# Weight taps and spectra on ScalarE's queue, x alone on SyncE's, and the gates' weight sums moved into the middle of the frequency phase

## The chip, the core and the metric

The kernel runs on one core of one Trainium2 chip. A core has five engines that run their own instruction streams in order and wait for one another through semaphores: TensorE (matrix products, PE in the profile), VectorE (DVE), ScalarE (ACT), GpSimd (POOL) and SyncE (SP), which only starts transfers. VectorE, ScalarE and GpSimd do elementwise work; SyncE and ScalarE can each start DMA transfers, and each has a DMA queue of its own. TensorE's results land in eight banks of PSUM, from which VectorE or ScalarE must copy them before a bank can be used again. The metric is the device time of one execution in microseconds (us); lower is better.

## What is computed

The input x is 128 graphs of 128 nodes with 256 channels. Only the first steps of the first layer touch the change:

```python
h = maximum(layernorm(x), 0)                    # per node
# inside the first layer, on h:
xc = transpose(h)                               # channels x nodes
c  = relu(bn1(conv1d(xc, conv1_w, pad=0)))      # 1-wide: a 256x256 product
c  = bn2(conv1d(c, conv2_w, pad=8))             # 17 taps over the nodes, 256 -> 256 channels
x_conv = transpose(relu(c + xc))
A = exp(-dist(h)) ; x_nmp = A @ relu(h @ w_msg + b_msg)
gi = concat(x_conv, x_nmp) @ w_ih.T ; gh = h @ w_hh.T
# a GRU cell on gi, gh; then x = x + result, and a second layer of five small graph convolutions
```

## The kernel before

**Blocks and halves.** The 128 graphs are worked on in 32 blocks of four (BB = 4), 16 blocks to a half. One block of x is 0.5 MB.

**The convolution by spectra.** The 17-tap convolution is done as a product in the frequency domain. A stretch of nodes is turned into 40 frequency pairs (LW = 80 values), and the 17 taps of each pair of channels too. For each pair p there is then one complex 256x256 product over all graphs of a half, written with three real products.

**The phases.** In order of time:

1. *Heads of half 0, interleaved with the weight spectra* (0 to 196 us). Eight weight spectra (2 parts of the input channels, 4 groups of 64 output channels) are made by `weight_spectra` in four steps each. In a step TensorE fills four PSUM banks (L160), of which ScalarE copies three (L168) and VectorE the fourth (L166) into the tile `sp`; after the fourth step `sp` (2.5 MB) is stored to `vd` in DRAM (L170). The taps of a spectrum are loaded by `taps_load` (L150) into the tile `w2`, 1 MB, of which there are two: those of spectrum k+2 can only be loaded when spectrum k has been through TensorE. Between the steps run the heads. For block i: its x load (L177, tile `ln`, five of them in half 0 and three in half 1), moments on VectorE (`head_stats`, L184, with a power on GpSimd at L189), normalisation on VectorE (`head_norm`, L195), transposes on TensorE (`head_turn`, L205, with relu to `ht` on ScalarE at L206, and a store `htd`, 0.5 MB, on ScalarE's queue at L207), the 1-wide convolution (`head_conv1`, L219; VectorE adds at L222, ScalarE does the relu at L223), and the transform to frequencies (`head_spectra`, L234; copies to X by VectorE at L240 and by ScalarE at L242).
2. *Frequency phase of half 0* (196 to 311 us), `spectral`: for each p, the spectra v are loaded from `vd` (L284, two loads of 0.5 MB for two frequencies, three such tiles), VectorE makes s (L297), GpSimd the sum vs of the real and imaginary parts (L299), TensorE does 12 matmuls (L302 and L307), ScalarE copies k1 (L304), VectorE adds (L308), and every four frequencies are stored to `yd` on ScalarE's queue.
3. *Heads of half 1* (311 to 426 us) and *frequency phase of half 1* (to about 540 us).
4. *The gates and the rest*, 540 us to the end.

**The gates' weight sums.** The gates use a product scheme with seven products in place of eight, for which sums of the blocks of the weights wih and whh are needed once, in `sw` and in place. `gate_weights` (L321 to L329) makes them as 12 additions on GpSimd; nothing needs them before the gates phase.

**What sets the order.** The program is written in one stream, and a scheduler with priorities gives each engine its own order when the kernel is built, and places the semaphores. An engine carries out its list in order, and a wait in it holds up what stands behind. Before the change, SyncE's order in the first phase is, for each spectrum k: the taps of k+2, the store of k, the x of block k+5. The 12 sums stand in GpSimd's order between vs of p = 3 and vs of p = 4.

Of the kernel before, what the change touches and what calls it, by code (L numbers as in the profile page):

```python
# [21 lines left out]
NP_ = LW // 2  # L22
WCH = 64
# [51 lines left out]
def gnn_kernel(ctx: ExitStack, tc: tile.TileContext, io, out0: bass.AP, out1: bass.AP):  # L75
    nc = tc.nc
# [15 lines left out]
    def bank():  # L92
        return psum.tile([P, 512], F32, tag="bank", name="bank")

    def row(name, n):

        return bass.AP(tensor=io[name].tensor, offset=io[name].offset, ap=[[0, P], [1, n]])
# [46 lines left out]
    vd = dram.tile([C, D // WCH, P, LW, WCH], F32, tag="vd", name="vd")  # L144
    yd = [dram.tile([HG, 2, LW, D], F32, tag=f"yd{h}", name=f"yd{h}") for h in range(NH)]

    def taps_load(pool, c, q, split=1):
        w2 = pool.tile([P, WCH // 4, P], F32, tag="w2", name="w2", bufs=2)
        for t in range(0, WCH // 4, WCH // 4 // split):
            nc.sync.dma_start(w2[:, t:t + WCH // 4 // split], io["w2t"][:, c, q, t:t + WCH // 4 // split])  # L150
        return w2

    def weight_spectra(pool, c, q, w2):

        sp = pool.tile([P, LW, WCH], F32, tag="sp", name="sp", bufs=2)
        for t in range(WCH // 16):
            ps = [bank() for _ in range(4)]
            for j in range(4):
                for r in range(4):
                    nc.tensor.matmul(ps[r][:, j * LW:(j + 1) * LW], w2[32 * r:32 * r + KW, 4 * t + j, :],  # L160
                                     gt[32 * r:32 * r + KW, :], start=True, stop=True)
            for r in range(4):
                o0 = t * 16 + 4 * r
                dst, s = sp[:, :, o0:o0 + 4], ps[r][:, :4 * LW].rearrange("p (j d) -> p d j", j=4)
                if r == 3:
                    nc.vector.tensor_copy(dst, s)  # L166
                else:
                    nc.scalar.copy(dst, s)  # L168
            yield
        nc.sync.dma_start(vd[c, q], sp)  # L170


    xs, stats, hcs, h1s = {}, {}, {}, {}
# [1 line left out]
    def head_load(pool, ahead, i, queue):  # L175
        xs[i] = pool.tile([P, BB, D], F32, tag="ln", name="ln", bufs=ahead)
        queue.dma_start(xs[i], x[i * BB:(i + 1) * BB].rearrange("b n d -> n b d"))  # L177
# [66 lines left out]
    def heads_begin(wk, xk, ahead, h):  # L244

        i = h * NBH
        for k in range(1 if h == 0 else 0, ahead):
            head_load(xk, ahead, i + k, nc.sync)
        for k in range(1 if h == 0 else 0, 3):
            head_stats(wk, i + k)  # L250
            if k < 2:
                head_norm(i + k)
        head_turn(wk, i)
# [20 lines left out]
    def spectral(bp, X, h, near_end):  # L274

        for p0 in range(0, NP_, 4):
            if p0 == NP_ - 8:
                near_end()
            ys = bp.tile([P, 4, 2, D], F32, tag="ys", name="ys", bufs=2)
            for p in range(p0, p0 + 4):  # L280
                if p % 2 == 0:
                    v = bp.tile([P, C, D // WCH, 4, WCH], F32, tag="v", name="v", bufs=3)
                    for c in range(C):
                        nc.sync.dma_start(v[:, c], vd[c, :, :, 2 * p:2 * p + 4, :].rearrange("q i d o -> i q d o"))  # L284
                vr, vi = v[:, :, :, 2 * (p % 2), :], v[:, :, :, 2 * (p % 2) + 1, :]
                a, d = X[:, :, p, 0, :], X[:, :, p, 1, :]
                y = ys[:, p - p0]
                ps = bank()
                if p == 0:
                    for k, (u, w) in enumerate(((a, vr), (d, vi))):  # L290
                        for c in range(C):
                            nc.tensor.matmul(ps[:, k * D:(k + 1) * D], u[:, c], w[:, c], start=c == 0, stop=c == C - 1)
                    nc.scalar.copy(y.rearrange("p k o -> p (k o)"), ps)
                    continue

                s = bp.tile([P, C, P], F32, tag="s", name="s", bufs=2)
                nc.vector.scalar_tensor_tensor(s, a, -2.0, d, op0=ALU.mult, op1=ALU.subtract)  # L297
                vs = bp.tile([P, C, D // WCH, WCH], F32, tag="vs", name="vs", bufs=3)
                nc.gpsimd.tensor_tensor(vs, vr, vi, op=ALU.add)  # L299
                p1 = bank()  # L300
                for c in range(C):
                    nc.tensor.matmul(p1[:, :D], a[:, c], vs[:, c], start=c == 0, stop=c == C - 1)  # L302
                k1 = bp.tile([P, D], F32, tag="k1", name="k1", bufs=2)
                nc.scalar.copy(k1, p1[:, :D])  # L304
                for k, (u, w) in enumerate(((s, vi), (d, vr))):
                    for c in range(C):
                        nc.tensor.matmul(ps[:, k * D:(k + 1) * D], u[:, c], w[:, c], start=c == 0, stop=c == C - 1)  # L307
                nc.vector.tensor_tensor(y, ps.rearrange("p (k o) -> p k o", k=2),  # L308
                                        k1[:, None, :].to_broadcast([P, 2, D]), op=ALU.add)
            for w in range(2):  # L310
                nc.scalar.dma_start(yd[h][:, w, 2 * p0:2 * p0 + 8, :].rearrange("g d o -> g (d o)"),
                                    ys[w * HG:(w + 1) * HG].rearrange("p a k o -> p (a k o)"))
# [18 lines left out]
    with front as es:  # L331
        hk = es.enter_context(tc.tile_pool(name="hk", bufs=1))
        xp = es.enter_context(tc.tile_pool(name="xp", bufs=1))
        X = xp.tile([P, C, NP_, 2, P], F32)
        with ExitStack() as ws:

            xk = ws.enter_context(tc.tile_pool(name="xk", bufs=1, side="right"))
            wp = ws.enter_context(tc.tile_pool(name="wp", bufs=1))
            ahead = 5
            todo = [(c, q) for c in range(C) for q in range(D // WCH)]  # L340
            head_load(xk, ahead, 0, nc.scalar)
            nc.sync.dma_start(gt, io["gt"])
            taps = [taps_load(wp, *todo[k], split=1 if k else 4) for k in range(2)]
            head_stats(hk, 0)
            head_norm(0)
            spectra = []

            def some_spectra(k=1):
                for _ in range(k):
                    if not spectra and todo:  # L350
                        spectra.append(weight_spectra(wp, *todo.pop(0), taps.pop(0)))
                    if spectra and next(spectra[0], STOP) is STOP:
                        spectra.pop(0)
                        if len(todo) > 1:
                            taps.append(taps_load(wp, *todo[1]))
                        some_spectra()

            some_spectra(3)
            constants()
            heads_begin(hk, xk, ahead, 0)  # L360
            some_spectra(3)
            heads(hk, xk, ahead, X, 0, lambda: some_spectra(2))
            while spectra or todo:
                some_spectra()
        gw = ctx.enter_context(tc.tile_pool(name="gw", bufs=1, side="right", reuse_waits="tile"))
        xk = es.enter_context(tc.tile_pool(name="xk1", bufs=1, reuse_waits="tile"))
        bp = es.enter_context(tc.tile_pool(name="bp", bufs=1, reuse_waits="tile"))
        idm = gw.tile([P, N], F32)
        wms = gw.tile([P, C, D + 3], F32)
        bms = gw.tile([P, D + 3], F32)  # L370
        wih = gw.tile([P, 2 * C, 3 * D], F32)
        whh = gw.tile([P, C, 3 * D], F32)
        sw = [gw.tile([P, 3, 3, P], F32, name=f"sw{k}") for k in range(3)]
        for h in range(NH):
            if h:
                heads(hk, xk, 3, X, h, lambda: None)
            spectral(bp, X, h, lambda: heads_begin(hk, xk, 3, h + 1) if h + 1 < NH else None)
            if h == 0:
                nc.sync.dma_start(idm, io["idm"])
                nc.sync.dma_start(wms, io["wms"].rearrange("(c p) o -> p c o", p=P))  # L380
                nc.sync.dma_start(bms, row("bms", D + 3))
                nc.sync.dma_start(fw, row("fw", 5))
                nc.sync.dma_start(wih, io["wih"].rearrange("(c p) o -> p c o", p=P))
                nc.sync.dma_start(whh, io["whh"].rearrange("(c p) o -> p c o", p=P))
                gate_weights()
# [718 lines left out]
```

## Time and profile before

Three runs took 1967.03, 1967.13 and 1971.97 us; the median is 1967.13 us. The profiled execution spans 1967.8 us.

| engine | busy us | share of the span |
|---|---|---|
| TensorE | 1911.4 | 97% |
| TensorE, weight loads | 1664.8 | 85% |
| VectorE | 1288.8 | 65% |
| ScalarE | 711.4 | 36% |
| GpSimd | 610.3 | 31% |

The share is an average over phases. TensorE is busy almost without a break from 540 us on; the page's second part, which cuts the span into 40 slices of 49.2 us, gives it 8, 8, 8 and 9 tenths in the first four slices and 7 in the seventh. In the same four slices the DMA engines are 8, 8, 8 and 5 tenths busy. In profile lines, a time in square brackets is how long the engine stood idle before the instruction, and the arrow names the instruction or the load that ended the wait. A row with "x4" joins four instructions of one kind. A row of SyncE's DMA queue (SPq) says when a transfer was started, not when it landed. TensorE's clock can be granted in full or in part; the same matmul then has a longer duration.

### The profile page before, as it was taken

Reading aid. Unit: us, or ns where it says so; the run is one execution under the profiler, and the core shown is the slowest. Engines: PE = TensorE matmul, PEld = TensorE weight load, DVE = VectorE, ACT = ScalarE, POOL = GpSimd, SP = SyncE. Lnnn points to the kernel's source line nnn. Section 1 sums busy time; section 2 is a strip of 40 time slices with the busy share of each in tenths; the row PEclk is TensorE's granted clock in tenths of the full one; section 3 lists DMA queues with packets and bytes.
Section 4 is the critical chain, followed back from the end, with each engine's and each line's share of the span. In section 5 each row is a group of like instructions: output and inputs, shape, how many; then the busy total and the mean of one; then the engine's idle time right before and its main releaser. Section 6 shows DMA issues by size and latency. Waiting matters only on the chain.

```text
span 1967.8 us, 29919 instructions
## 1 busy us (share of the span) xinstructions
PE 1911.4 (97%) x10418; PEld 1664.8 (85%) x10418; DVE 1288.8 (65%) x3255; ACT 711.4 (36%) x1438; POOL 610.3 (31%) x681
## 2 busy tenths in 40 slices
PE   8889997999999999999999999999999999999998
PEld 7778886998878888888878888888878888888887
DVE  6556445855468777777756677777756677777643
ACT  4444112531133433433434433333434433333334
POOL 1011641115423344344322143343322143343300
PEclk9899998999999999999999999999999999999999
DMA  8885795439863323323423533322423533322135
GB/s 312 324 290 179 229 314 183 164 123 293 282 197 84 90 67 92 89 69 79 121 59 98 129 107 83 95 71 70 123 71 94 130 94 94 84 71 56 51 90 148
DMA packets 248853, 265.76 MB, mean 135 GB/s; under 512 B 106850, under 2 KB 223927, under 8 KB 244223
## 3 DMA queue, kind: packets, MB, share of 16 engines
q1 hardware_dynamic: 240367, 225.58, 39.6%
q10 hardware_dynamic: 8336, 38.28, 5.1%
q8 instruction: 83, 1.36, 0.3%
q14 instruction: 67, 0.55, 0.1%
HBM read 178.66 MB, written 85.14 MB: 134 GB/s over the span
## 4 chain that ended last, share of the span: by engine, by line
PE 89%; DMA 5%; DVE 3%; POOL 1%; issue 1%; ACT 1%; SPq 0%; POOLq 0%; DVEq 0%; ACTq 0%
PE bank L565 44%; PE bank L307 6%; PE bank L471 6%; PE bank L884 5%; PE bank L824 5%; PE bank L219 5%; PE bank L302 3%; PE bank L517 3%; PE bank L453 3%; DMA ln<-in_x_dram 3%; PE bank L234 2%; PE bank L456 1%; PE bank L504 1%; PE bank L803 1%; PE bank L735 1%; PE bank L205 1%
## 5 line engine op out<-in xcount | busy, mean ns | idle before, releaser
L565 PE MATMUL bank<-t,sw 128*128 128x256 f32 x1152 | 290.7, 379 | 0.0
L578 POOL TENSOR_TENSOR u<-u,m 128x256 f32<-128x256 f32 x128 | 93.0, 726 | 595.2 <-ACT m L576 546.3
L565 PEld LDWEIGHTS bank<-t,sw 128*128 128x128 f32 x1152 | 215.6, 190 | 29.7 <-issue 2.3
L565 PE MATMUL bank<-t,wih 128*128 128x256 f32 x768 | 197.2, 379 | 0.0
L565 PEld LDWEIGHTS bank<-t,wih 128*128 128x128 f32 x768 | 143.4, 190 | 19.3 <-DVE u L583 0.5
L219 PE MATMUL bank<-wc,ht 128*128 128x256 f32 x512 | 130.0, 411 | 13.9 <-ACT ht L206 13.2
L299 POOL TENSOR_TENSOR vs<-v 128x512 f32<-128x512 f32 x78 | 101.1, 1315 | 130.1 <-DMA v<-vd 73.7
L219 PEld LDWEIGHTS bank<-wc,ht 128*128 128x128 f32 x512 | 103.7, 207 | 32.1 <-ACT ht L206 16.3
L471 PE MATMUL bank<-wms,ht 128*128 128x259 f32 x512 | 122.3, 381 | 0.0
L884 PE MATMUL bank<-w,hh 128*125 128x256 f32 (+9 forms) x480 | 113.6, 380 | 1.0 <-DVE hh L829 1.0
L565 PE MATMUL bank<-t,whh 128*128 128x256 f32 x384 | 114.4, 379 | 0.0
L565 PE MATMUL bank<-xn,wih 128*128 128x256 f32 x384 | 114.2, 379 | 0.0
L565 PE MATMUL bank<-xc,wih 128*128 128x256 f32 x384 | 114.2, 379 | 0.0
L297 DVE SCALAR_TENSOR_TENSOR s<-X 128x256 f32<-128x256 f32 x78 | 52.5, 675 | 91.9 <-PE bank L307 91.7
L565 PE MATMUL bank<-ht,whh 128*128 128x256 f32 x384 | 110.2, 381 | 0.0
L471 PEld LDWEIGHTS bank<-wms,ht 128*128 128x128 f32 x512 | 97.2, 190 | 14.6
L824 PE MATMUL bank<-ax,w 128*128 128x500 f32 (+8 forms) x416 | 107.0, 396 | 0.2 <-DMA w<-in_w_dram 0.2
L583 DVE TENSOR_TENSOR u<-bank,u 128x256 f32<-128x256 f32 x128 | 53.7, 419 | 74.0 <-PE bank L565 74.0
L189 POOL TENSOR_TENSOR rs<-ve,mhalf 128x4 f32<-128x4 f32 x32 | 32.3, 1009 | 225.2 <-DVE ve L187 225.2
L884 PEld LDWEIGHTS bank<-w,hh 128*125 128x125 f32 (+9 forms) x480 | 84.3, 178 | 19.3 <-DVE hh L829 1.6
L475 ACT ACTIVATE msg<-msg 128x512 f32<-128x512 f32 x64 | 40.3, 630 | 162.6 <-DVE msg L472 160.2
L304 ACT COPY k<-bank 128x256 f32<-128x256 f32 x78 | 28.9, 372 | 178.6 <-DVE ys L308 69.8
(190 smaller groups left out, 4307.1 us busy)
## 6 DMA issues: line engine op xcount, KB each, us to landing
v<-vd SPq DMA_DIRECT2D x80, 512.0 KB
vd<-sp SPq DMA_DIRECT2D x8, 2560.0 KB
yd<-ys ACTq DMA_DIRECT2D x40, 512.0 KB
w<-in_w_dram SPq DMA_DIRECT2D x40, 512.0 KB
htd<-ht ACTq DMA_DIRECT2D x32, 512.0 KB
ht<-htd SPq DMA_DIRECT2D x32, 512.0 KB
ym<-yd SPq DMA_DIRECT2D x32, 512.0 KB
xt<-in_xT_dram SPq DMA_DIRECT2D x32, 512.0 KB
```

Of the source, the lines that this page charges most:

```text
L219: nc.tensor.matmul(pv[:, bb, :], ht[:, c, b * N:(b + 1) * N], wc1[:, c, :], start=c == 0, stop=c == C - 1)
L299: nc.gpsimd.tensor_tensor(vs, vr, vi, op=ALU.add)
L302: nc.tensor.matmul(p1[:, :D], a[:, c], vs[:, c], start=c == 0, stop=c == C - 1)
L307: nc.tensor.matmul(ps[:, k * D:(k + 1) * D], u[:, c], w[:, c], start=c == 0, stop=c == C - 1)
L453: nc.tensor.matmul(ps[:, b * N:(b + 1) * N], ym[:, b, o * P:(o + 1) * P], idm, start=b == 0, stop=False)
L471: nc.tensor.matmul(ps[:, :D + 3], ht[:, c, b * N:(b + 1) * N], wms[:, c, :], start=c == 0, stop=c == C - 1)
L517: nc.tensor.matmul(ps[:, b * N:(b + 1) * N], msg[:, b, c * P:(c + 1) * P], e[:, b, :], start=True, stop=True)
L565: nc.tensor.matmul(ps, w, d, start=n == 0, stop=n == len(pairs) - 1)
L578: nc.gpsimd.tensor_tensor(got["u4"], got["u2"], got["m5"], op=ALU.add)
L583: nc.vector.tensor_tensor(got["u3"], ps, got["u2"], op=ALU.add)
L824: nc.tensor.matmul(pv[:, q - q0, :], w1s[k5 + g][:, c, q * P:(q + 1) * P], xv[:, c], start=c == 0, stop=c == C - 1)
L884: nc.tensor.matmul(ps[:n1, :D], hh[:, q, at:at + n1], w2s[k5 + g][:, q, :], start=q == 0, stop=q == HID // P - 1)
```

## The change

Four edits belong together.

1. `taps_load` is given a queue. The first two taps stay on SyncE, the other six go on ScalarE's queue.
2. The store of a spectrum goes on ScalarE's queue too. In the last step of each spectrum (t = 3) ScalarE now makes all four copies, so that the store on its queue waits for no copy by VectorE.
3. The first three x loads of half 1 go on ScalarE's queue. SyncE thus has x alone in the heads of half 0, and the loads of v behind it.
4. In half 0, at p = 20, three copies of one column of k1 into the tiles `sw` are put on GpSimd. The sums write the same elements, so they can only follow; this is a way to tell the scheduler that the sums come after p = 20. The columns are written over by the sums.

The aim of 1 to 3 is that an x block does not queue behind taps and stores; the aim of 4 is that the sums do not stand at the head of the frequency phase.

As built, SyncE's order has the x of blocks 1 to 13, the six loads of v for p = 0 to 5, and then the x of block 14. ScalarE's order has, per spectrum, the seven remaining copies, the two relu of `ht`, the store of the spectrum, the store `htd`, and the taps of the spectrum after next. GpSimd's order has vs of p = 25, the three copies, nine sums, vs of p = 26, two sums, vs of p = 27, and the last sum.

```diff
-    def taps_load(pool, c, q, split=1):
+    def taps_load(pool, c, q, queue, split=1):
         w2 = pool.tile([P, WCH // 4, P], F32, tag="w2", name="w2", bufs=2)
         for t in range(0, WCH // 4, WCH // 4 // split):
-            nc.sync.dma_start(w2[:, t:t + WCH // 4 // split], io["w2t"][:, c, q, t:t + WCH // 4 // split])
+            queue.dma_start(w2[:, t:t + WCH // 4 // split], io["w2t"][:, c, q, t:t + WCH // 4 // split])
...
-                if r == 3:
+                if r == 3 and t < WCH // 16 - 1:
                     nc.vector.tensor_copy(dst, s)
                 else:
                     nc.scalar.copy(dst, s)
             yield
-        nc.sync.dma_start(vd[c, q], sp)
+        nc.scalar.dma_start(vd[c, q], sp)
...
         for k in range(1 if h == 0 else 0, ahead):
-            head_load(xk, ahead, i + k, nc.sync)
+            head_load(xk, ahead, i + k, nc.scalar if h else nc.sync)
...
                 nc.scalar.copy(k1, p1[:, :D])
+                if h == 0 and p == NP_ // 2:
+
+                    for t in sw:
+                        nc.gpsimd.tensor_copy(t[:, 0, 1, 0:1], k1[:, 0:1])
...
-            taps = [taps_load(wp, *todo[k], split=1 if k else 4) for k in range(2)]
+            taps = [taps_load(wp, *todo[k], nc.sync, split=1 if k else 4) for k in range(2)]
...
-                            taps.append(taps_load(wp, *todo[1]))
+                            taps.append(taps_load(wp, *todo[1], nc.scalar))
```

## The prediction

> **What bounds the kernel now.** The page's first part has TensorE busy 97% of 1967.8 us. From about 540 us on, none of the changed lines runs, and TensorE has no gaps worth the name. So I read the first 310 us: first the table of 50 us stretches, whose columns are busy time and instruction count of each engine, granted clock, DMA share and GB/s.
>
> ```profile
> 0.00:50.00 50.00, 40.19 (x517) 35.44 (x518) 30.48 (x116) 21.55 (x54) 9.51 (x19) 0.93 0.90 311
> 50.00:100.00 50.00, 44.05 (x528) 39.04 (x527) 26.05 (x84) 23.37 (x67) 3.06 (x4) 0.86 0.86 328
> 100.00:150.00 50.00, 42.99 (x396) 38.30 (x395) 27.49 (x85) 21.88 (x58) 6.51 (x6) 0.93 0.81 288
> 150.00:200.00 50.00, 45.60 (x254) 40.31 (x253) 33.84 (x111) 19.40 (x53) 11.69 (x13) 0.93 0.45 160
> ```
>
> TensorE is idle 23 us of the first 150 while the transfers run at 0.8 to 0.9. To name the wait I took the timelines of TensorE and VectorE at one hole.
>
> ```profile
> 64.28 2.01 PE L160 MATMUL bank<-gt,w 17*128 17x80 f32 x32 [4.02 <-DVE sp L166]
> 66.22 4.23 PE L234 MATMUL bank<-fd,h 128*128 128x160 f32 x16
> ...
> 109.57 2.01 PE L160 MATMUL bank<-gt,w 17*128 17x80 f32 x32 [4.08 <-DVE sp L166]
> ```
>
> ```profile
> 62.09 0.75 DVE L184 BATCH_NORM_STATS2 st<-ln 128x6 f32<-128x256 f32 x2 [4.31 <-DMA ln<-in_x_dram]
> ...
> 63.76 0.46 DVE L166 COPY sp<-bank 128x320 f32<-128x320 f32 x1
> ```
>
> TensorE waits for a bank, the bank for VectorE's copy, and that copy stands in VectorE's order behind the moments of an x block that has not landed. Why it is late stands in SyncE's queue, then in the chain of waits:
>
> ```profile
> 91.21 0.33 SPq L150 DMA_DIRECT2D w<-in_w2t_dram  x1
> 92.92 0.33 SPq L170 DMA_DIRECT2D vd<-sp  x1
> 93.34 0.39 SPq L177 DMA_DIRECT2D ln<-in_x_dram  x1
> 109.58 0.33 SPq L170 DMA_DIRECT2D vd<-sp  x1
> 110.00 0.39 SPq L177 DMA_DIRECT2D ln<-in_x_dram  x1
> ```
>
> ```profile
> 93.34 14.03 DMA ln<-in_x_dram
> 107.39 0.75 DVE st L184 x2
> 110.00 9.79 DMA ln<-in_x_dram
> ```
>
> 0.5 MB of x needs 14.0 us behind taps and store, 9.8 us behind a store alone. Last, the sums of the gates' weights (GpSimd, then TensorE):
>
> ```profile
> 194.73 1.96 POOL L326 TENSOR_TENSOR sw<-wih 128x384 f32<-128x384 f32 x2 [17.10 <-DMA wih<-in_wih_dram]
> ...
> 207.51 4.92 POOL L299 TENSOR_TENSOR vs<-v 128x512 f32<-128x512 f32 x4
> ```
>
> ```profile
> 208.82 1.14 PE L302 MATMUL bank<-vs,X 128*128 128x256 f32 x4 [2.79 <-POOL vs L299]
> 209.79 1.88 PE L307 MATMUL bank<-v,s 128*128 128x256 f32 x4
> ...
> 214.07 1.03 PE L307 MATMUL bank<-v,s 128*128 128x256 f32 x4
> ```
>
> Twelve sums stand ahead of vs of p=4; TensorE waits 2.79 us and then works at about half rate until 213.18.
>
> **What the Trainium skill says.** "TensorE: Matmul & The Clock Gate", Part 1 (The HAM clock gate): an idle window of about 3.4 us halves the array's clock until a busy one. The trace agrees on the halving (L307 1.88 against 1.03 us, L234 4.23 against 2.34), but here a hole of 2.79 us is enough; I price a hole of 2.5 us or more with 2 us on top. The same page (Architectural detail) has ScalarE and VectorE as strict FIFOs; the copy at 63.76 agrees. "DMA: Bandwidth & Descriptors", Queues, rings and completion order: SyncE and ScalarE each own one ring per DMA engine, read in ring order, and an engine takes turns between rings. The trace agrees on ring order, with x landing after taps and store; that x alone on its ring then passes a store on the other, no run here shows yet. Its Bandwidth section gives 425 GB/s for large loads; here 3.14 MB (store and x) took 10.2 us and 4.72 MB (with taps and htd) 14.5, so I use 2.2 us plus 2.55 us per MB, or 392 GB/s.
>
> **The change, part by part.**
>
> *x alone on SyncE, last copy on ScalarE.* With five x buffers and its own ring, x comes early, and the holes at 64.28 and 109.57 go: 4.0 + 4.1 plus 2 us of clock each, 12 us. The two smaller waits on L166 near 80 and 95 (0.6 each) go too. The copies moved cost VectorE 8 x 0.48 us less and ScalarE 8 x 0.44 us more; ScalarE is at half load. Both are hidden.
>
> *Taps and store on ScalarE.* Before, taps k+2 were issued when the taps' buffer came free, 1.7 us ahead of store k (91.21 and 92.92). In the changed order of ScalarE they stand behind store k and htd. A clean cycle (92.03 to 104.22) is 12.2 us; counted from step 0 of a spectrum, its store is issued 14 us later (11.2 to the end of step 3, 1.8 of copies, about 1 for the two ht that ScalarE does ahead). Behind it the taps bring 2.62 + 0.52 + 1.05 MB: 2.2 + 2.55 x 4.19 = 12.9 us, up to 14.2 if an x shares the time; I take 13.5. They are due at 24.4 us and land at 27.5, so two cycles take 27.5 and one 13.75 us, against 14.7 before (22.15 to 125.04 in seven). Behind the waiting TensorE stand all head matmuls. The changed order of VectorE also puts the moments and norms of x4 and x5 ahead of a copy of the second spectrum, so that its store goes out near 38 instead of 35.85. The eighth store: 38 + 6 x 13.75 = 120.5, against 125.04, **4.5 us gained**. If taps came in time it would be 38 + 6 x 13 = 116, as 4.72 MB a cycle at 392 GB/s take 12.0 us and need some slack; if each taps hole also costs 2 us of clock, (16 + 13.5)/2 = 14.75 and 126.5. Bounds: -9 to +1.5.
>
> *From the eighth store to the frequency phase (71.3 us before).* A head needs 6.5 us there (174.96 to 181.46); between 138 and 168 11.4 us are lost, as x12 to x15 come late and VectorE bunches. After, x12 and x13 are early, but on SyncE the x of block 14 now stands behind all six v loads, the second of which waits for the eighth store to land, 10 us after its issue; five more half-megabytes and itself land 25 us after it. VectorE reaches its moments 14 to 20 us after, ahead of the addition of h(9), and blocks. TensorE has some 3 us of other heads' work, so 6 to 8 us are lost, 3 more in bunching: 10, **1.4 gained**; bounds -4 to +5. The three x loads put on ScalarE wait in its order for a landed store and htd, about 2.8 us twice, beside a busy TensorE: nothing.
>
> *Sums.* The wait at 208.82 goes: 2.79 + 1.8 of clock, **4.6 gained**. But three copies and nine sums now stand between vs of p=25 and p=26. Before (GpSimd):
>
> ```profile
> 258.48 2.68 POOL L299 TENSOR_TENSOR vs<-v 128x512 f32<-128x512 f32 x2 [1.29 <-DMA v<-vd]
> 265.05 2.49 POOL L299 TENSOR_TENSOR vs<-v 128x512 f32<-128x512 f32 x2 [3.89 <-DMA v<-vd]
> ```
>
> vs of 25 ends at 261.16; TensorE wants 26 at 267.59, so GpSimd has 3.89 us to spare and no more, being fed by pairs of v. The sums take 12.8/12 = 1.07 us each (194.73 to 207.51), nine 9.6. A 128x1 copy has no row: between 0 and the 0.7 us of the 128x2 power; I take 0.7 for all three. 261.16 + 0.7 + 9.6 + 1.27 = 272.7: a hole of 5.1 us, plus 1.8 of clock; the other three sums hide behind the slow clock. **6.9 lost**, net 2.3; bounds of the net -1 to +5, the lower end if v comes earlier than before.
>
> Sum: -4.5 - 1.4 + 2.3 = -3.6, and 1967.1 - 3.6 = **1963.5 us**. The waits for x19 and x20 (295 to 324) keep their order on SyncE and stay.
>
> **The rivals.** *Taps in time*: the other ring is fast enough once x is off it. For it: DMA share is 0.86, not 1, and x passes through while nothing else runs. Against: a 12.2 us cycle wants 387 GB/s. -9 - 3 + 2.3: 1957. *The new waits take all*: every taps hole halves the clock, block 14's x stalls longer, sums cost their full hole. For: 2.79 us was enough to halve the clock. Against: the two 4 us holes do go. +1.5 + 4 + 4: 1977, slower. *Sums hidden after all*, the spectra as forecast: GpSimd would have to run ahead by three vs; the lead of 1.3 us at p=26 (266.3 to 267.59) speaks against it. -4.5 - 1.4 - 4.6: 1956.5.
>
> **How the numbers follow.** Forecast 0.42, taps in time 0.2, sums hidden 0.08, new waits 0.26, something beyond 0.04. With a scatter of 5 us the forecast, 2.3 us above the 0.3% line of 1961.2, gives 0.14 faster, 0.26 the same, 0.02 slower; the first two rivals are faster, the third slower. So 0.43, 0.28, 0.29. The range goes from taps in time with its lower bounds to just past the slower rival: 1951 to 1979.
>
> **What would show it.** Right: TensorE's waits on L166 at step 3 gone; instead waits of 1 to 2 us on a w2t load in front of a spectrum; the eighth store at about 120; VectorE waiting for one x some 25 us after it; no hole at p=4, and one of about 5 us at p=26 behind the sums. Wrong: stores less than 13 us or more than 14.7 apart, or vs of p=26 in time. Most doubtful are the stretch after the eighth store, where four engines wait in order on one another, and how short a hole halves the clock.

## The result, and the profile after

The changed kernel takes 2022.95 us (median of 4 runs, 2020.96 to 2024.51) against 1968.46 for the kernel before in the same comparison: a ratio of 1.0274, 95% interval 1.0255 to 1.0292. It is 54 us slower. The forecast was 1963.5, the slower rival 1977, the upper end of the range 1979.

The stretches of 50 us of the changed kernel, with the same columns as before:

```profile
0.00:50.00 50.00, 32.93 (x368) 29.24 (x368) 24.88 (x100) 17.13 (x40) 8.56 (x18) 0.86 0.75 271
50.00:100.00 50.00, 28.81 (x318) 24.49 (x319) 15.90 (x54) 14.95 (x41) 2.19 (x3) 0.64 0.40 160
100.00:150.00 50.00, 39.68 (x429) 33.81 (x428) 18.31 (x55) 17.41 (x49) 2.85 (x3) 0.75 0.61 241
150.00:200.00 50.00, 41.86 (x312) 36.26 (x311) 19.00 (x64) 17.19 (x48) 6.79 (x6) 0.83 0.78 281
```

Everything fell together: TensorE, VectorE, ScalarE and the transfers (DMA share 0.40 in the second stretch against 0.86), and the granted clock. No engine became the bound. Engines that are all idle at once wait for one another, so the thing to read is the chain of waits, here of the changed kernel in one cycle:

```profile
92.00 1.04 PE bank L205 x8
93.05 4.32 DMA ln<-in_x_dram
97.39 0.75 DVE st L184 x2
...
98.93 0.39 DVE sp L166
...
99.83 1.02 POOL rs L189
100.87 0.41 DVE ln L195
101.28 0.48 DVE X L240 x2
101.89 2.47 PE bank L234 x8
104.36 5.20 PE bank L219 x16
...
112.58 4.47 DMA ln<-in_x_dram
```

It is a loop. The transposes (L205) free an x buffer, the next x is started at once, and VectorE waits for it. Behind its moments stand two things that TensorE needs: the copy of a bank into `sp` (L166) and, behind the power on GpSimd and the first normalisation, the copy of a bank into X (L240). Then TensorE goes on through the transform and the 1-wide convolution to the next transposes. The turn shown takes 19.5 us, from 93.05 to 112.58; the two ahead of it took 24.7 and 28.8. The order of VectorE shows why it can wait there. Before (between the step 2 and step 3 copies, 12.6 us after that x was started, at 78.12):

```profile
90.33 0.49 DVE L166 COPY sp<-bank 128x320 f32<-128x320 f32 x1 [0.48 <-PE bank L160]
90.74 0.74 DVE L184 BATCH_NORM_STATS2 st<-ln 128x6 f32<-128x256 f32 x2
...
92.40 0.46 DVE L166 COPY sp<-bank 128x320 f32<-128x320 f32 x1
```

and changed (between the copies of steps 0 and 1, right behind the start of x at 93.05):

```profile
94.32 0.49 DVE L166 COPY sp<-bank 128x320 f32<-128x320 f32 x1 [2.58 <-PE bank L160]
97.39 0.75 DVE L184 BATCH_NORM_STATS2 st<-ln 128x6 f32<-128x256 f32 x2 [2.59 <-DMA ln<-in_x_dram]
...
98.85 0.47 DVE L166 COPY sp<-bank 128x320 f32<-128x320 f32 x1
```

The holes on TensorE, changed kernel:

```profile
55.77 3.78 PE L219 MATMUL bank<-wc,ht 128*128 128x256 f32 x8 [9.11 <-DVE sp L166]
...
80.77 1.44 PE L234 MATMUL bank<-fd,h 128*128 128x160 f32 x4 [11.54 <-DVE sp L166]
...
99.38 1.43 PE L234 MATMUL bank<-fd,h 128*128 128x160 f32 x4 [2.76 <-DVE sp L166]
```

The account, from one profiled execution of each (L292 is the first matmul of p = 0):

| stage | before | changed | difference |
|---|---|---|---|
| to the issue of the eighth store | 125.0 | 171.3 | +46.3 |
| from there to the first L292 of the frequency phase | 71.3 | 77.8 | +6.5 |
| frequency phase of half 0 | 115.0 | 121.3 | +6.3 |
| the rest | 1656.5 | 1650.0 | -6.5 |

Of the last row, 4.9 us lie behind the second frequency phase, where no changed line runs; in the 18 profiled executions of this document that part takes 1433.0 to 1437.9 us, so it is scatter as far as is known. The moved x loads of half 1 were not run alone; the stretch between the two frequency phases took 114.2 us before and 113.9 changed.

### The profile page after: what moved, and what is told of

Same layout as the page of the kernel before. It is cut to its first block, busy times and chain, and to the rows that moved or that the text cites. A ratio compares the mean times of both kernels' runs of the same rounds, so it can differ in the third digit from the quotient of the medians.

```text
span 2020.4 us, 29902 instructions
## 1 busy us (share of the span) xinstructions
PE 1927.2 (95%) x10418; PEld 1676.5 (83%) x10418; DVE 1281.9 (63%) x3247; ACT 716.1 (35%) x1446; POOL 609.9 (30%) x684
## 4 chain that ended last, share of the span: by engine, by line
PE 86%; DMA 6%; DVE 4%; POOL 1%; issue 1%; ACT 0%; SPq 0%; POOLq 0%; DVEq 0%; ACTq 0%
PE bank L569 42%; PE bank L311 6%; PE bank L475 5%; PE bank L888 5%; PE bank L828 5%; PE bank L219 5%; DMA ln<-in_x_dram 3%; PE bank L302 3%; PE bank L521 3%; PE bank L457 3%; PE bank L234 3%; DMA v<-vd 2%; PE bank L460 1%; PE bank L508 1%; PE bank L807 1%; PE bank L205 1%
## 5 line engine op out<-in xcount | busy, mean ns | idle before, releaser
L219 PE MATMUL bank<-wc,ht 128*128 128x256 f32 x512 | 136.5, 426 | 26.7 <-ACT ht L206 15.9
L219 PEld LDWEIGHTS bank<-wc,ht 128*128 128x128 f32 x512 | 108.9, 218 | 46.8 <-ACT ht L206 18.5
L234 PE MATMUL bank<-fd,h 128*128 128x160 f32 x512 | 87.0, 325 | 29.5 <-DVE sp L166 24.1
L569 PE MATMUL bank<-xn,wih 128*128 128x256 f32 x384 | 114.2, 379 | 0.0
L569 PE MATMUL bank<-xc,wih 128*128 128x256 f32 x384 | 114.2, 379 | 0.0
L234 PEld LDWEIGHTS bank<-fd,h 128*128 128x128 f32 x512 | 78.6, 207 | 33.3 <-DVE sp L166 25.5
```

Source lines behind the costliest of these rows:

```text
L219: nc.tensor.matmul(pv[:, bb, :], ht[:, c, b * N:(b + 1) * N], wc1[:, c, :], start=c == 0, stop=c == C - 1)
L234: nc.tensor.matmul(ps[:, bb * 2 * LW:(bb + 1) * 2 * LW], h1[:, 2 * h + bb, c * P:(c + 1) * P], fd, start=True, stop=True)
L569: nc.tensor.matmul(ps, w, d, start=n == 0, stop=n == len(pairs) - 1)
```

## The experiments

Ratios are to the kernel before in the same comparison, with 95% intervals. "The eighth store" is the time of its issue in the profiled execution.

**s1, the sums alone.** The kernel before with the added lines of `spectral` only.

> The kernel before with the fourth edit alone (the three copies at p = 20, so the sums stand behind it). Theory: the hole at p = 4 is not removed but taken over by the wait for v of p = 8 (about 4.6 us with the clock), because the sums had only hidden the landing of v, and the new hole at p = 26 costs about 6.8 us: 1974 to 1976 us, 6 to 8 slower than before. Rival, the prediction: hole at p = 4 gone, net +2.3, 1970 us.

1966.65 us, ratio 0.9995 (0.9985 to 1.0004). My theory after the result was wrong. The frequency phase took 117.7 us against 115.0: hole at p = 4 gone, and at p = 26

```profile
263.61 2.08 PE L302 MATMUL bank<-vs,X 128*128 128x256 f32 x4 [4.08 <-POOL vs L299]
```

That is +2.7 in the phase, near the prediction's net of +2.3. The total shows no loss over 14 runs. In the profiled execution everything ahead of the frequency phase was 3.5 us shorter than before, and it is 1.7 and 4.0 us shorter in s8 and s11, which also move the sums away from the head; whether moving them causes that is not shown.

**s2, the changed kernel without the sums' edit.**

> The changed kernel without the fourth edit: queues and the last copy alone. Theory: the whole loss in the heads of the first half stays, less the 6.5 us of the sums: 2015 to 2018 us. Rival: the edits act on one another and more than 10 us come back: under 2012 us.

2018.78 us, 1.0276 (1.0247 to 1.0306), eighth store at 171.1: a little above what I expected, at the ratio of the whole change. The loss is in the other edits, and the totals show none by the sums.

**s3, the moments back in their place.**

```diff
+            if t == 2:
+                marks[c * (D // WCH) + q] = sp
             yield
...
         st = wk.tile([P, BB, 6], F32, tag="st", name="st", bufs=2)
+        if 5 <= i <= 11:
+            nc.vector.tensor_copy(st[:, :, 0:1], marks[i - 4][:, 0:4, 44:45])
```

> The changed kernel with both queues as they are, but the moments of blocks 5 to 11 tied behind VectorE's copy of step 2 of the spectrum (a copy of four columns of sp into st ahead of them, which the moments overwrite), where they stood before the change. Theory of the order: the stores go out 12 to 15 us apart again in place of 19.5, the eighth near 125, total 1968 to 1982 us. Rival, the queues (store, htd and taps on ScalarE's ring hold up x, ScalarE or the taps): no more than 10 us come back, over 2010 us.

1988.15 us, 1.0109 (1.0085 to 1.0133). Same queues in the same order, and 33 to 35 of the 54 us are back (by the ratios and by the times): stores 16.7 us apart, the eighth at 136.8. The order is shown as the main cause; the time is still outside what I expected, so something else costs 12 us up to the eighth store.

**s4, six x buffers.** `ahead = 6`.

> The changed kernel with six buffers for x in place of five. Theory of the order: the build moves the moments of the block loaded a head earlier up along with its load, so VectorE still waits for a load just started: 2005 to 2025 us. Rival, too few buffers: x is there a head early, the waits on the sp copies vanish, 1965 to 1985 us.

2020.97 us, 1.0275 (1.0254 to 1.0297). Another buffer does not help: as built, the moments move up with the load, and VectorE waits for a load just started. The chain has the same loop:

```profile
63.58 14.84 DMA ln<-in_x_dram
79.98 0.39 DVE sp L166
93.74 4.59 DMA ln<-in_x_dram
99.89 0.39 DVE sp L166
```

**s5, only the store; s6, only the taps.** Each on ScalarE's queue with the last copies, without the sums' edit, the other transfer back on SyncE.

> The changed kernel with the taps back on SyncE and the sums back at the head: only the store and the last copies on ScalarE. In VectorE's order as built the moments of a block then stand behind the step 1 copy, one copy later than in the changed kernel, so TensorE waits for the copies of X and not for those of sp. Theory of the order: part of the loss comes back, eighth store at 130 to 155, 1975 to 2000 us. Rival, the taps behind the store make the cycle: 1960 to 1972 us.

2032.78 us, 1.0334 (1.0305 to 1.0362): even slower than all edits together, a miss. The moments stand one copy later, but ahead of the copies of X, and x, now behind the taps, lands later. The chain:

```profile
84.20 15.68 DMA ln<-in_x_dram
99.90 0.75 DVE st L184 x2
100.66 0.47 DVE X L240 x2
101.26 2.47 PE bank L234 x8
```

> The changed kernel with the store back on SyncE and the sums back at the head: only the taps and the last copies on ScalarE. As built, the moments stand ahead of the step 2 copy, nearly where they stood before the change. Theory of the order: the eighth store at 118 to 130, 1960 to 1975 us. Rival, taps late or their issue holding up ScalarE: eighth store after 135, over 1980 us.

1973.01 us, 1.0034 (1.0022 to 1.0046), as expected. The taps on ScalarE, with the last copies, cost 4 to 9 us; the profiled execution, with the eighth store at 125.9, is the fastest of eleven and does not show where. Of the two moves it is the store's that brings the moments forward.

**s7, the last copy alone.** `if r == 3 and t < WCH // 16 - 1:` in the kernel before.

> The kernel before with the last copy of each spectrum on ScalarE alone, all queues as before. Theory: the two holes of 4 us, which waited for the step 3 copy by VectorE behind the moments, go, 5 to 12 us faster: 1955 to 1963 us. Rival: x is as late as ever, and the same wait moves to the next copy, the one of step 0: within 3 us of before.

1965.95 us, 1.0005 (0.9993 to 1.0017). The rival holds: the wait on VectorE's copy went from the spectra (L160) to the transform (L234).

```profile
80.65 4.63 PE L234 MATMUL bank<-fd,h 128*128 128x160 f32 x16 [3.98 <-DVE sp L166]
```

**s8, the sums in pairs.** In the kernel before, behind the copy to k1:

```diff
+                if h == 0 and p % 4 == 0 and 8 <= p <= 28:
+                    t, j = sw[(p - 8) // 8], 1 if p % 8 == 0 else 0
+                    nc.gpsimd.tensor_copy(t[:, 0, j, 0:1], k1[:, 0:1])
```

> The kernel before with the sums spread in pairs behind p = 8, 12, 16, 20, 24 and 28 by the same kind of copy. Theory: both holes are gone, that at p = 4 and that at p = 26, about 4 us faster than before and 6 faster than with the sums at p = 20: 1961 to 1965 us. Rival, v is late at p = 8 or later without the hole: 1967 us.

1956.30 us, 0.9957 (0.9941 to 0.9974), faster than both kernels and by more than I expected. Neither hole is left. In the profiled execution the frequency phase is 3.8 us shorter than before; where the rest of the gain lies was not traced. A pair fits into GpSimd's slack of 3 to 4 us (L307 is the small copy, L331 and L332 are sums):

```profile
231.03 2.68 POOL L299 TENSOR_TENSOR vs<-v 128x512 f32<-128x512 f32 x2 [1.13 <-DMA v<-vd]
233.65 0.19 POOL L307 COPY sw<-k 128x1 f32<-128x1 f32 x1
233.92 1.00 POOL L331 TENSOR_TENSOR sw<-wih 128x384 f32<-128x384 f32 x1
234.99 1.16 POOL L332 TENSOR_TENSOR sw<-wih,sw 128x384 f32<-128x384 f32 x1
237.78 2.49 POOL L299 TENSOR_TENSOR vs<-v 128x512 f32<-128x512 f32 x2 [1.63 <-DMA v<-vd]
```

**s9, taps ahead of the store.** s3, with the load of the next taps started before the store in `weight_spectra`. As built, the store `htd` then also goes ahead of the store of the spectrum, as long as there are taps to load.

> The changed kernel with the moments tied as before, and in ScalarE's order the taps ahead of the store and htd. Theory: the 16.7 us a cycle of the tied kernel are left because ScalarE starts the copies of step 0 only once it has issued store, htd and taps, of which the taps take 1.4 us behind a full ring against 0.33; issued first they take 0.33, the hole before L234 falls from 1.3 to under 0.5 us, the clock stays up, and a cycle takes 14 to 15 us: eighth store at 118 to 128, total 1968 to 1978. Rival: VectorE's chain of moments, power and normalisation ahead of the step 0 copy makes the cycle, 16 to 17 us, total 1984 to 1990.

1987.41 us, 1.0098 (1.0083 to 1.0112), eighth store at 136.9. My theory fell. Starting the taps did shrink (0.39 us against 1.3 to 2.3), and the wait stayed. One cycle:

```profile
102.61 2.92 PE L160 MATMUL bank<-gt,w 17*128 17x80 f32 x64
106.87 2.50 PE L240 MATMUL bank<-fd,h 128*128 128x160 f32 x8 [1.33 <-DVE sp L166]
110.11 2.47 PE L240 MATMUL bank<-fd,h 128*128 128x160 f32 x8 [0.74 <-DVE X L246]
```

(L240 is the transform and L246 VectorE's copy to X, L234 and L240 elsewhere.) The tie itself, a small copy on VectorE and the wait behind it, takes about 0.5 us of the cycle. The built programs say where the waits come from. PSUM banks are dealt out when the kernel is built; this is what the four banks of one head's transform wait for:

```
kernel before                changed, s3 and s9
ScalarE's copy, step 0       VectorE's copy, step 0
VectorE's copy, step 0       VectorE's copy, step 1
ScalarE's copy, step 0       VectorE's copy of X, second bank of the same head
ScalarE's copy, step 0       ScalarE's copy, step 0
```

The semaphores in the traces name the same engines, in the same order.

**s10, blocks 14 and 15 past the loads of v.** s9, with the x of these two on ScalarE's queue.

> The same with the x of blocks 14 and 15 on ScalarE's queue, and so not behind the six loads of v. Theory: the 6 us lost between the eighth store and the frequency phase come back (77.7 to about 71 us between them), 4 to 8 us faster than with the taps first alone. Rival: VectorE's own work bunches there whatever x does, less than 2 us faster.

1981.58 us, 1.0073 (1.0057 to 1.0088), 5.8 us faster than s9. From the eighth store to the frequency phase 72.9 us against 78.1: this is where 5.2 of the +6.5 of the account came from.

**s11, v behind block 15, in s8.** A column of block 15's moments copied into each half of the first three v tiles ahead of their loads.

> The kernel before with the sums in pairs, and the first six loads of v tied behind the moments of block 15 (a copied column that the load overwrites), so that the last x blocks do not share the transfers with v. Theory: half or more of the 11 us that the heads lose between 138 and 168 us comes back: 1946 to 1953 us. Rival: the loads of v are not what made x12 to x15 late, 1955 to 1959 us as with the sums in pairs alone.

1958.26 us, 0.9951 (0.9937 to 0.9966): the rival. With the loads of v started behind all x loads of the half no time is gained, so they are not what costs the heads time in the kernel before.

**s12, all mendings on the changed queues.** s9 with the pairs of s8 and the tie of s11.

> The changed kernel's queues with all four mendings: moments tied, taps ahead of the store, sums in pairs, v tied behind block 15. Theory: 1950 to 1965 us, faster than before. Rival: ScalarE's queue costs the spectra more than SyncE's order did, over 1968 us.

1975.83 us, 1.0039 (1.0024 to 1.0054): the rival; the cycles of 15 to 20 us, 16.8 in the mean, remain.

**s13, no spectrum copy on VectorE.** s9 with `nc.scalar.copy(dst, s)` for all four copies of every step.

> The kernel with moments tied and taps first, with all copies of sp on ScalarE, so that no bank of the spectra waits for VectorE. Theory of chain and banks: the wait in front of the transforms goes, a cycle takes 12.5 to 15 us, eighth store at 110 to 125, total 1962 to 1977 us. Rival, ScalarE's queue or its load (now 16 copies a cycle and three transfers to start): 16.5 us a cycle or more, over 1984 us.

1974.49 us, 1.0037 (1.0025 to 1.0049), eighth store at 121.4, from the third store on 12.4 to 15.6 us apart. Twelve to thirteen us come back against s9, so the rest of the loss up to the eighth store hung on VectorE's copies of `sp`: they stand behind its chain of moments, power and normalisation, and banks wait behind them. How much is the chain and how much the dealing of the banks is not told apart. The same stretch of a cycle as for s9, without the waits (L237 is the transform here, L222 the 1-wide convolution):

```profile
93.00 3.40 PE L160 MATMUL bank<-gt,w 17*128 17x80 f32 x64
96.50 3.84 PE L237 MATMUL bank<-fd,h 128*128 128x160 f32 x16
100.18 3.62 PE L222 MATMUL bank<-wc,ht 128*128 128x256 f32 x16
```

**s14, the same on the changed kernel as it is, moments early.**

> The changed kernel as it is, moments early, with all copies of sp on ScalarE. Theory: VectorE still waits for an x just started, but of what stands behind, TensorE needs only the copies of X and the addition of h: half or more of the 46 us up to the eighth store come back, eighth store at 120 to 150, 1970 to 2000 us. Rival: the loop from turn through x to TensorE goes on through the copies of X as with the store alone, over 2010 us.

2038.63 us, 1.0365 (1.0351 to 1.0378), a miss for the theory as I put it. The loop only needs one thing behind the moments that TensorE wants; here it is the copy of X (L237 in this kernel):

```profile
110.48 1.80 PE L160 MATMUL bank<-gt,w 17*128 17x80 f32 x28 [6.86 <-DVE X L237]
```

So s13 and s14 are to be read together: with the moments late, taking the copies of `sp` off VectorE helps; with the moments early it does not.

**s15 and s16, the search for a better kernel.** s15 is s8 with all copies on ScalarE, s16 is s12 with the same.

> The kernel before with the sums in pairs and all copies of sp on ScalarE. Theory: no hole waits for a copy by VectorE, so the two holes of 4 us go, 1946 to 1954 us. Rival: ScalarE becomes the bound of the spectra or x's lateness shows at the next wait, 1955 us or more.

1953.23 us, 0.9930 (0.9913 to 0.9948): the fastest median of all, some 70 us under the changed kernel, with SyncE's queue as it was. The eighth store is at 115.9, the last four cycles take 13.7 us each, and the two holes of 4 us are gone. Its interval still meets that of s8.

> The changed kernel's queues with moments tied, taps first, sums in pairs, v tied behind block 15, all copies of sp on ScalarE. Theory: with the waits gone the queues of the change pay at last, 1945 to 1958 us. Rival: no better than the kernel before with the same mendings.

1960.64 us, 0.9963 (0.9950 to 0.9976): the rival; the queues of the change, with all these mendings, are still behind, by 0.3%.

## Why the prediction was wrong

- **"With five x buffers and its own ring, x comes early, and the holes at 64.28 and 109.57 go": the step that failed.** It has two faults. x cannot come early, because its buffer is only freed by the transposes of the same cycle; SyncE started it at 39.52, 64.25 and 93.05, 0.1 to 0.7 us ahead of the store, where before it was 0.4 us behind, and with the shorter lead it took 14.2 and 14.5 us to land. And VectorE's order was held fixed. The build put the moments of every block right behind the start of its load. I had seen that for x4 and x5 and priced it with 2 us, once; it held for the blocks from x6 to x11, and turned a landing time that had been hidden in most cycles into a part of each. In place of 4.5 us gained, the eighth store came 46.3 us later. s3 shows 33 to 35 us for the order.
- **That the build does this because it reckons x to land soon on an empty queue** is argued, not shown. Shown is only that moving the store brings it (s5, s6) and that the last copy does not (s7).
- **"The taps are due at 24.4 us and land at 27.5"**: no run tests it in this form. Its rate was read too fast: the 14.5 us for 4.72 MB were counted from the store at 92.92, but the taps among them had been started at 91.21. In the changed kernel no wait on a w2t load is left but the first, because cycles of 18 to 29 us leave time enough, and at some 13.8 us (s13) there is none either, with the taps ahead of the store.
- **"The copies moved … both are hidden"**: right about engine time (s7: no change), blind to the banks. With the store on ScalarE, two of the four banks of a head's transform hang on VectorE's copies and one on its copy of X: 2 us of waits in the cycle shown for s9, none in that of s13.
- **The stretch after the eighth store**: the mechanism, block 14 behind v, was right, its size was not. x14 landed 31 us after the store, not 25, and the stretch grew by 6.5 us where 1.4 were to be gained. The chain of the changed kernel:

```profile
171.31 9.99 DMA vd<-sp
181.32 9.81 DMA v<-vd
191.19 11.15 DMA ln<-in_x_dram
```

s10 gives 5.2 us back by taking that x out of the queue.

- **The sums**: right in mechanism, and near in size within the frequency phase (s1: +2.7 for +2.3; at p = 26 a hole of 4.1 us for 5.1), but the totals of s1 and s2 show no net loss. The three small copies took 0.41 us for 0.7. In the changed kernel the phase is 4.8 us longer than in s2 (121.3 against 116.5), since the hole at p = 4 came back at p = 8, where GpSimd had waited 9.13 us for v:

```profile
271.86 2.08 PE L302 MATMUL bank<-vs,X 128*128 128x256 f32 x4 [2.67 <-POOL vs L299]
```

That v was started at 259.31 and took 11.1 us; why it did and not in s1 stays open.

- **The slower rival** had 0.26 and ended at 1977: it knew that new waits could take all, and looked for them in taps, clock and sums, not in the order of VectorE.

## What to carry to other kernels

Where a scheduler sets each engine's order at build time, moving a transfer to another queue can also change the order of other engines and the dealing of the banks, as it did here: compare the built orders line by line before pricing anything. The question to ask of an order is how far a load's first user stands behind its start, and what the other engines need behind that user; here a move ahead of two copies cost 33 to 35 us. And work that only has to be done some time (the sums) goes best in portions of the slack it is to fill: as one block it cost a hole in both places tried, in pairs none.

## What the runs showed of the hardware

- **A queue of its own doesn't give a transfer its share.** In the changed kernel x was started at 64.25 and a store on the other queue 0.09 us later; x needed 14.51 us, as long as the whole group. At 93.05 it was 0.70 us ahead and needed 4.32.

```profile
64.34 0.33 ACTq L170 DMA_DIRECT2D vd<-sp  x1
...
93.75 0.33 ACTq L170 DMA_DIRECT2D vd<-sp  x1
```

The Trainium skill ("DMA: Bandwidth & Descriptors", Queues, rings and completion order) says that an engine takes turns between rings packet by packet. The trace agrees, and shows why such turns are no equal share. From 67 to 72 us the two queues got nearly the same number of packets, but a packet of the store (queue q10, ScalarE's) has 20 KB and one of x (q1, SyncE's) 1 KB. The columns are packets, MB and the share of the 16 DMA engines' time:

```profile
q10 hardware_dynamic: 104, 2.13, 99.1%
q1 hardware_dynamic: 105, 0.11, 6.6%
```

What differed was the lead. The first packet of the x started at 64.25 moved 0.8 us ahead of the store's first; that of the x started at 93.05 moved 2.3 us ahead, and most of this x was through when the store began.

- **Starting a load can hold up the engine that starts it.** Taps started on ScalarE behind store and htd took 1.3 to 2.3 us, ahead of them 0.39 or less (s9), where the store behind them took up to 1.48; on SyncE 0.33.
- **Holes and the clock.** A hole of 2.79 us was followed by about half rate in the kernel before, one of 2.99 us in s6 was not (the L302 behind it took 1.13, and the L307 1.03 us). The stretches at half clock that the traces record begin and end on a grid of 3.41 us: in the kernel before they are 3.41, 6.83 or 10.24 us long, but for the last, which the end of the execution cuts off. Here are the pieces of that grid around the two holes, first the kernel before, then s6; behind the width stand TensorE's busy time and matmuls, third from the end the granted clock:

```profile
206.40:209.81 3.41, 0.99 (x5) 0.88 (x6) 0.43 (x1) 0.00 (x0) 3.33 (x4) 1.00 0.74 213
209.81:213.22 3.41, 3.41 (x10) 2.65 (x9) 1.00 (x1) 0.37 (x1) 2.62 (x3) 0.50 1.04 373
```

```profile
206.79:210.20 3.41, 1.50 (x7) 0.97 (x6) 1.32 (x2) 0.18 (x1) 3.23 (x4) 1.00 0.39 122
210.20:213.61 3.41, 2.33 (x11) 2.07 (x12) 0.30 (x1) 0.37 (x1) 3.41 (x3) 1.00 1.00 308
```

The shorter hole emptied most of one piece, the longer one lay across two. That agrees with the free-running window of the Trainium skill ("TensorE: Matmul & The Clock Gate", Part 1): the length alone does not decide. How much work in a window is enough was not measured. My flat 2 us per hole was a mean at best.
